# Turned shares and key shifts in one PSUM bank, shares ahead of numbers, batch norm in one ScalarE step

## The chip, the core and the metric

One core of a Trainium2 chip runs the kernel. Its engines are TensorE (PE, with the weight load PEld beside it), VectorE (DVE), ScalarE (ACT), GpSimd (POOL) and SyncE (SP), which here only issues transfers. The metric is the device time of one execution in microseconds (us), as the median of several runs. A profile is one further execution, recorded by the hardware profiler.

## The reference

```python
x = L0_attn_x                                         # 16 x 512 x 128
x = x + attention(layernorm(x), w_qkv, w_proj)        # 16 heads of 8, window of 128
y = layernorm(x)                                      # input of the experts
mu, var = mean(y, 0), mean((y - mu) ** 2, 0)          # over all 8192 tokens
q = ((y - mu) * rsqrt(var + 1e-5) * gamma + beta) @ w_q.T
sim = einsum('pbnhd,hkpd->pbnhk', q, keys)            # 8 heads, 2 x 32 keys
s, i = top_k(sim, 8)                                  # for both halves of the keys
scores, pk = top_k(sx[:, None] + sy[None, :], 8)      # 8 of the 64 sums
idx = take(ix * 32 + iy, pk)                          # 8 of 1024 experts a head
o = gelu(y . key_in[idx]) * softmax(scores)
return x + sum(o * key_out[idx])
```

## The kernel before, in words

The first part is the windowed attention of the sixteen batches, followed by the second layer norm, whose transposed output goes to DRAM. The change doesn't touch it.

The second part starts with the batch norm: `bn_aggr` (L547) gives mean and variance of each of the 128 features, L549 to L551 make `bn_a` = gamma / sqrt(var + eps), a value for each partition.

Then come the experts. A batch has 512 tokens, in four tiles of 128, so there are 64 turns of the main loop (L872); turn i works on tile t = i mod 4 of batch b. The order of instructions on each of the four compute engines is written out by hand: `InOrder` (its calls all carry line L577) keeps every engine's instructions in the order of the program text. The loop overlaps three turns: it finishes turn i - 1, works on i, and begins i + 1. In one turn:

- `where_keys` (sixteen MAX8 and FIND_INDEX8 results of the two key halves of 8 heads), `best_sums` and `where_sums` (L674) find the eight best sums of each head and the place of each among 64. `where_sums` splits the place into `upper` and `shift`: two VectorE steps for each, on 64 elements a partition.
- `pick_words` (L693) picks the word that holds the key's number on GpSimd; `share_of` (L700) makes the softmax shares: VectorE sums and inverts, GpSimd multiplies (`share`).
- `numbers` (L709) shifts `word` by `shift` on VectorE and takes three fields out of it (`num`, three VectorE steps). It stands between the first four and the last twelve of the sixteen MAX8 of turn i + 1 (`best_keys`, L630).
- `turn` (L719) casts `num` to bf16 on ScalarE and turns shares and numbers round on TensorE, so that choices lie on partitions: two fp32 matmuls for the shares into columns 2, six bf16 ones into columns 0 and 1 of `x_ps`. ScalarE then copies `p_bf` and `wT` out.
- `other_ones_of_p` (L766), `ones_of_c` (L744), `weights_at_c` (L752) and `ones_of_p` (L759) build one-hot rows (`row`) and weighted columns (`mine`, `cols`) on ScalarE, VectorE and GpSimd; `weigh` (L781) multiplies them on TensorE into `w_ps`, the weight of every expert for every token.
- `take_weights` and `weigh_experts` multiply these by the GELU of `down`; `up` (L807) multiplies the product by `key_out`.

`fill(i, 0)` and `fill(i, 1)` (L851) put the matmuls of other batches between: in odd turns `down` of the batch that follows, with its GELUs on ScalarE; in even turns `up` of a batch that came before. `fill(i, 0)` stands ahead of `where_sums`, so its matmuls are ahead of `turn`'s in TensorE's queue. `scale` (L594) applies the batch norm to a batch, at the end of turn t = 2 of the batch before.

`x_ps` is in the pool `ps_t` (L562), one buffer of one PSUM bank; VectorE reads it in `ones_of_c` and `ones_of_p`.

Of the kernel before, what the change touches and what calls it, by code (L numbers as in the profile page):

```python
# [10 lines left out]
F32 = mybir.dt.float32  # L11
BF16 = mybir.dt.bfloat16
I32 = mybir.dt.int32
U32 = mybir.dt.uint32
U8 = mybir.dt.uint8
AF = mybir.ActivationFunctionType
ALU = mybir.AluOpType
# [3 lines left out]
P = 128  # L21
# [22 lines left out]
def kernel(  # L44
# [13 lines left out]
    nc = tc.nc  # L58
# [12 lines left out]
    const = ctx.enter_context(tc.tile_pool(name="const", bufs=1))  # L71
# [9 lines left out]
    for b in range(B):  # L81
        t = keep.tile([P, NQ, D], F32, name=f"x_{b}")
# [3 lines left out]
    gb = const.tile([P, 2], F32, name="gb")  # L86
# [8 lines left out]
    ident = const.tile([P, P], F32, name="ident")  # L95
    make_identity(nc, ident)
    ident_bf = const.tile([P, P], BF16, name="ident_bf")
# [42 lines left out]
    xts = {}  # L140

    def load(b):
        xts[b] = ahead.tile([P, T], F32, tag="xt", name=f"xt_{b}")
        nc.sync.dma_start(xts[b], xT[b])
# [8 lines left out]
    with ExitStack() as at:  # L153
# [280 lines left out]
        def weigh(n, u):  # L434

            b, g = divmod(n, NG)
            ts = near(u)
            q0, w = ts[0] * P, len(ts) * P
            pT = probs.pop((n, u))
            if u == 0:  # L440
                outs[n] = ps_o.tile([P, T], F32, tag="o", name=f"o_ps_{n}")
            for j in range(4):
                mm(
                    outs[n][32 * j : 32 * j + 32, q0 : q0 + w], lhsT=vaug[b % 3][:, u, 4 * g + j],
                    rhs=pT[:, j, 0:w], start=u == 0, stop=u == NQ - 1, skip_group_check=True,
                )
            if u == NQ - 1:
                oT = w2.tile([P, T], F32, tag="oT", name=f"oT_{n}")
                nc.scalar.copy(oT, outs[n])
                outs[n] = oT  # L450
# [46 lines left out]
        for s in range(-2 * NG * NQ, (NU + 1) * NQ):  # L497
            n, u = divmod(s, NQ)
            b, g = divmod(n, NG)
# [46 lines left out]
    bn_mv = const.tile([P, 2], F32, name="bn_mv")  # L546
    nc.vector.bn_aggr(bn_mv, bn_st.rearrange("p b s -> p (b s)"))  # L547
    bn_a = const.tile([P, 1], F32, name="bn_a")
    nc.scalar.activation(bn_a, bn_mv[:, 1:2], AF.Sqrt, bias=eps)  # L549
    nc.vector.reciprocal(bn_a, bn_a)  # L550
    nc.vector.tensor_mul(bn_a, bn_a, gb[:, 0:1])  # L551

# [2 lines left out]
    b2 = ctx.enter_context(tc.tile_pool(name="b2", bufs=2))  # L557
# [4 lines left out]
    ps_t = ctx.enter_context(tc.tile_pool(name="ps_t", bufs=1, space=PSUM))  # L562
    HK = H * TOPK
    HT, QT = P // 2, P // 4
    NM = QT // 2
    HM = NM // 2
    halves = [slice(v * HT, v * HT + HT) for v in range(2)]
# [11 lines left out]
    pe, dve, act, pool = (InOrder(e) for e in (nc.tensor, nc.vector, nc.scalar, nc.gpsimd))  # L579
# [9 lines left out]
    xbs, downs, gels, gs, ups, outs_T = {}, {}, {}, {}, {}, {}  # L589
    sims, tops, cands, idxs, bytes_of, steps_of = {}, {}, {}, {}, {}, {}  # L590
    bests, ws, shares, places, shifts, words, nums, turned = {}, {}, {}, {}, {}, {}, {}, {}
    mines, rows, weights = {}, {}, {}

    def scale(b):  # L594
        xb = b2.tile([P, T], F32, tag="xb", name=f"xb_{b}")
        dve.tensor_scalar(xb, xts[b], bn_mv[:, 0:1], bn_a, ALU.subtract, ALU.mult)
        act.activation(xb, xb, AF.Identity, bias=gb[:, 1:2])
        xbs[b] = xb

    def down(b, k):  # L600
# [16 lines left out]
    def score(j):  # L617
        b, t = divmod(j, NQ)
        sims[j] = ps_x.tile([P, 2 * H, NK], F32, tag="x", name=f"sim_ps_{j}")
        pe.matmul(  # L620
            sims[j].rearrange("p c k -> p (c k)"), lhsT=xbs[b][:, t * P : (t + 1) * P], rhs=wsim,
            start=True, stop=True,
        )

    def take_scores(j):
        sim = b2.tile([P, 2 * H, NK], F32, tag="sim", name=f"sim_{j}")
        act.copy(sim, sims[j])
        sims[j] = sim
# [16 lines left out]
    def where_keys(j):  # L645
        idx = b2.tile([P, H, 2, TOPK], U32, tag="idx", name=f"idx_{j}")
        sim, top = sims.pop(j), tops.pop(j)
        for c in range(2 * H):
            dve.max_index(idx[:, c // 2, c % 2], top[:, c // 2, c % 2], sim[:, c])
        idxs[j] = idx  # L650
# [23 lines left out]
    def where_sums(j):  # L674
        place = b2.tile([P, H, TOPK], U32, tag="place", name=f"place_{j}")
        best, cand = bests.pop(j), cands.pop(j)
        for h in range(H):
            dve.max_index(place[:, h], best[:, h], cand[:, h].rearrange("p a b -> p (a b)"))

        place = place.rearrange("p h k -> p (h k)")  # L680
        upper = b2.tile([P, 2, HK], U32, tag="upper", name=f"upper_{j}")
        shift = b2.tile([P, 2, HK], U32, tag="shift", name=f"shift_{j}")
        for i, right in enumerate((5, 2)):
            dve.tensor_scalar(
                upper[:, i], place, right, 1, ALU.logical_shift_right, ALU.bitwise_and
            )
        places[j], shifts[j] = upper, shift
        for i, left in enumerate((0, 3)):
            dve.tensor_scalar(
                shift[:, i], place, left, 24, ALU.logical_shift_left, ALU.bitwise_and  # L690
            )
# [8 lines left out]
    def share_of(j):  # L700
# [5 lines left out]
        pool.tensor_tensor(share, w, bc(zs, 2, TOPK), ALU.mult)  # L706
        shares[j] = share

    def numbers(j):  # L709

        key = words.pop(j).rearrange("p s h k -> p s (h k)").bitcast(U32)
        dve.tensor_tensor(key, key, shifts.pop(j), ALU.logical_shift_right)
        num = b2.tile([P, 3, HK], U32, tag="num", name=f"num_{j}")
        dve.tensor_scalar(num[:, 0], key[:, 0], NK - 1, 5, ALU.bitwise_and, ALU.logical_shift_left)
        dve.tensor_scalar(num[:, 1], key[:, 1], NC, None, ALU.bitwise_and)
        dve.tensor_scalar(num[:, 2], key[:, 1], NC - 1, None, ALU.bitwise_and)
        nums[j] = num

    def turn(j):  # L719

        num = b2.tile([P, 3, HK], BF16, tag="num_bf", name=f"num_bf_{j}")
        act.copy(num, nums.pop(j))
        x_ps = ps_t.tile([P, 3, HT], F32, tag="t", name=f"x_ps_{j}")
        share = shares.pop(j).rearrange("p h k -> p (h k)")
        for i, (to, what, eye) in enumerate((
            (2, share, ident), (0, num[:, 0], ident_bf), (0, num[:, 1], ident_bf),
            (1, num[:, 2], ident_bf),
        )):
            for v in range(2):
                pe.matmul(  # L730
                    x_ps[halves[v], to], lhsT=what, rhs=eye[:, halves[v]],
                    start=i == 0, stop=i != 1, skip_group_check=True,
                )
        p_bf = b2.tile([P, HT], BF16, tag="p_bf", name=f"p_bf_{j}")
        act.copy(p_bf, x_ps[:, 0])
        wT = b2.tile([P, HT], F32, tag="wT", name=f"wT_{j}")
        act.copy(wT, x_ps[:, 2])
        turned[j] = x_ps, p_bf, wT

    def some(t, m, rows_of=slice(0, P)):  # L740

# [52 lines left out]
    def take_weights(j, m):  # L794
        b, t = divmod(j, NQ)
        if t == m == 0:
            gs[b] = b2.tile([P, NC, NQ, 2, QT], F32, tag="g", name=f"g_{b}")
        g = gs[b][:, :, t, :, m * NM : m * NM + NM]
        act.copy(g, weights.pop((j, m)).rearrange("p n (s c) -> p c s n", s=2))
# [72 lines left out]
    for i in range(NB + 1):  # L872
        b, t = divmod(i, NQ)
        now, before, behind = i < NB, i > 0, i + 1 < NB
        if now:
            where_keys(i)
            if t == 0 and 0 < b < B - 1:
                load(b + 1)
        if behind:
            score(i + 1)  # L880
        if before:
            take_weights(i - 1, 0)
            weigh(i - 1, 1)
        if now:
            pack_keys(i)
        if behind:
            take_scores(i + 1)
        if now:
            best_sums(i)
            less_greatest(i)  # L890
        if before:
            weigh_experts(i - 1, 0)
            take_weights(i - 1, 1)
        if i == 0:
            for k in range(3, 8):
                down(0, k)
                gelu(0, k)
        if t == 1 and b > 1:
            finish(b - 2)
        fill(i, 0)  # L900
        if now:
            where_sums(i)
            pick_words(i)
            share_of(i)
        if t == 1 and b > 1:
            store(b - 2)
        if before:
            weigh_experts(i - 1, 1)
        if not now:
            break  # L910
        tops_of = best_keys(i + 1) if behind else iter(())
        next(tops_of, None)
        numbers(i)
        for _ in tops_of:
            pass
        turn(i)
        other_ones_of_p(i, 0)
        ones_of_c(i)
        if behind:
            sums_of_keys(i + 1)  # L920
        weights_at_c(i, 0)
        ones_of_p(i, 0)
        other_ones_of_p(i, 1)
        ones_of_p(i, 1)
        weights_at_c(i, 1)
        fill(i, 1)
        weigh(i, 0)
        if t == 2 and b + 1 < B:
            scale(b + 1)
# [41 lines left out]
```

## Time and profile before

| | |
|---|---|
| median of 3 runs | 1741.71 us (1736.61 to 1748.68) |
| the profiled execution: time, span | 1729.36 us, 1727.7 us |
| granted TensorE clock in it | 0.971 |
| busy over the span | PE 1447.6, PEld 851.4, DVE 1414.8, ACT 1175.8, POOL 1138.2 us |
| busy from 837.0 us to the end (890.7 us) | PE 752.7, PEld 522.4, DVE 835.5, ACT 657.2, POOL 605.4 us |
| `row<-x_ps,nums_p` on DVE | 128 times, 1214 ns each |
| `mine<-x_ps,nums_c` on DVE | 64 times, 1225 ns each |
| `upper<-place` on DVE | 128 times, 295 ns each |
| `cols<-mine,wT` on POOL | 256 times, 1066 ns each |
| `g<-g,gel` on POOL | 128 times, 1296 ns each |
| `wT<-x_ps` on ACT | 64 times, 218 ns each |
| `xb<-xt,bn_mv,bn_a` on DVE | 16 times, 589 ns each |
| `xb<-xb,gb` on ACT | 16 times, 705 ns each |

How to read it: a row of the profile names the line (L577 for all that `InOrder` records, so tiles tell them apart), the engine, the operation, what it writes and reads (`out<-in`), its shapes and types, and how often (x). In a list of groups, behind the bar, stand the busy time in us and the mean in ns of one, and then the idle time of the engine just before them with the releaser that ended it. In a timeline the first two columns are the start and the time taken, in us from the start of the span; neighbours of one kind are merged into one row. A list of waits has the waiting engine and tile, whom it waited for, and the total in us, the number of waits and the longest. In the page's slices each digit is a fortieth of the span in tenths of busy time, or, for PEclk, of the full clock that was granted.

### The profile page before, as it was taken

To read this page: it belongs to the slowest core of one execution; us is meant where nothing else is said; L and a number is where in the kernel's file an instruction comes from. 1 tells how busy PE (TensorE), PEld (TensorE's weight loads), DVE (VectorE), ACT (ScalarE), POOL (GpSimd) and SP (SyncE) were. 2 spreads that over 40 slices of the span, in tenths; PEclk is the share of its full clock that TensorE was granted. 3 is DMA by queue.
4 is the path that set the end of the run, shared out by engine and by line. 5 is a ranking of instruction groups with operands and counts; after the bars stand their busy time and mean duration, and the time that the engine had idled before them with its cause. 6 is when DMAs were issued, how large, how long until landed. Compare 5 with 4: busy or idle time off the path is not lost.

```text
span 1727.7 us, 49763 instructions
## 1 busy us (share of the span) xinstructions
PE 1447.6 (84%) x16752; PEld 851.4 (49%) x16752; DVE 1414.8 (82%) x7959; ACT 1175.8 (68%) x2530; POOL 1138.2 (66%) x1762
## 2 busy tenths in 40 slices
PE   4789898798788898898678888888888888888887
PEld 1344443344344443443345656565565655655655
DVE  3767777677776776684599999899999999999994
ACT  1466667666666666667577777777777777777773
POOL 9556557865577557646376766676767777676764
PEclk9799999999999999999899999899999999999998
DMA  6242222222222222221000000000000000000000
GB/s 168 70 112 83 72 76 65 81 75 72 69 72 82 76 71 68 78 70 38 20 8 2 14 14 9 14 8 15 14 8 15 8 15 14 9 15 8 8 9 14
DMA packets 87567, 75.05 MB, mean 43 GB/s; under 512 B 12176, under 2 KB 83088, under 8 KB 87184
## 3 DMA queue, kind: packets, MB, share of 16 engines
q1 hardware_dynamic: 86480, 71.61, 14.0%
q8 instruction: 133, 2.18, 0.5%
q14 instruction: 122, 1.00, 0.2%
q10 hardware_dynamic: 832, 0.26, 0.1%
HBM read 49.28 MB, written 20.97 MB: 41 GB/s over the span
## 4 chain that ended last, share of the span: by engine, by line
PE 35%; DVE 24%; ACT 22%; POOL 6%; SPq 6%; issue 4%; DMA 3%; DVEq 0%; ACTq 0%; POOLq 0%
PE s_ps L168 6%; PE o_ps L168 6%; PE w_ps L577 6%; ACT row L577 5%; DVE masked L379 4%; ACT off_p L577 4%; SPq L354 4%; PE e_ps L168 4%; ACT L577 3%; PE sim_ps L577 3%; DVE idx L577 3%; DVE num L577 3%; PE dn_ps L577 3%; DVE row L577 3%; ACT pT L421 3%
## 5 line engine op out<-in xcount | busy, mean ns | idle before, releaser
L379 DVE CUSTOM_DVE_ANT_0 masked<-s_ps,band 128x384 bf16<-128x384 f32 (+1 forms) x1024 | 498.8, 487 | 215.0 <-PE s_ps L168 83.2
L421 ACT ACTIVATE pT<-e_ps 128x384 f32<-128x384 f32 (+1 forms) x1024 | 389.5, 436 | 161.1 <-PE e_ps L168 156.9
L428 POOL TENSOR_SCALAR_AFFINE_SELECT pT<-pT 128x512 f32<-128x512 f32 x384 | 236.7, 635 | 232.6 <-ACT pT L421 228.1
L168 PE MATMUL s_ps<-kst,qst 128*128 128x384 bf16 (+1 forms) x1024 | 312.5, 308 | 36.4 <-DVE mx L379 17.8
L577 PEld LDWEIGHTS w_ps<-cols,row 128*64 128x64 f32 x8192 | 256.2, 140 | 90.9 <-POOL cols L577 38.1
L577 POOL TENSOR_TENSOR cols<-mine,wT 64x512 f32<-64x512 bf16 x256 | 272.9, 1066 | 35.3 <-DVE mine L577 22.0
L577 PE MATMUL w_ps<-cols,row 128*64 128x32 f32 x8192 | 266.3, 224 | 22.5 <-POOL cols L577 20.6
L168 PE MATMUL e_ps<-qst,kst 128*128 128x384 bf16 (+1 forms) x1024 | 230.3, 304 | 14.7 <-ACT pT L421 12.4
L168 PEld LDWEIGHTS <-qst 128*128 128x128 bf16 x1024 | 101.1, 99 | 211.3 <-issue 165.7
L168 PE MATMUL o_ps<-pT,vaug 128*32 128x384 f32 (+1 forms) x2048 | 193.4, 450 | 13.1 <-POOL pT L428 12.9
L577 ACT ACTIVATE row<-off_p,one 128x512 f32<-128x512 bf16 x256 | 184.8, 722 | 8.3
L577 ACT ACTIVATE off_p<-off_ps 128x512 bf16<-128x512 f32 x256 | 149.0, 582 | 37.9 <-PE off_ps L577 37.9
L577 POOL TENSOR_TENSOR g<-g,gel 128x512 f32<-128x512 f32 x128 | 165.9, 1296 | 5.1 <-ACT g L577 5.1
L577 DVE FIND_INDEX8 idx<-top,sim 128x8 uint32<-128x32 f32 x1024 | 166.2, 184 | 0.0
L577 DVE TENSOR_TENSOR row<-x_ps,nums_p 128x1024 f32<-128x1024 f32 x128 | 150.0, 1214 | 0.0
L577 PE MATMUL dn_ps<-xt,key_inT 128*64 128x256 f32 x1024 | 128.8, 396 | 20.8 <-ACT off_p L577 19.4
L577 PE MATMUL off_ps<-p_bf,ident_bf 128*128 128x512 bf16 x256 | 100.2, 391 | 46.5 <-ACT off_p L577 27.0
L577 POOL TENSOR_TENSOR cand<-top 128x512 f32<-128x512 f32 x64 | 68.1, 1065 | 98.2 <-DVE top L577 98.2
L577 PE MATMUL up_ps<-g,key_out_sb 64*128 64x256 f32 x1024 | 126.8, 388 | 0.0
L168 PEld LDWEIGHTS <-kst 128*128 128x128 bf16 x1024 | 98.1, 98 | 55.5 <-issue 29.1
L577 DVE MAX8 top<-sim 128x8 f32<-128x32 f32 x1024 | 104.5, 171 | 3.6 <-ACT sim L577 3.6
L577 PEld LDWEIGHTS dn_ps<-xt,key_inT 128*64 128x64 f32 x1024 | 70.2, 141 | 70.9 <-ACT off_p L577 34.2
(141 smaller groups left out, 2461.2 us busy)
## 6 DMA issues: line engine op xcount, KB each, us to landing
qst<-qv SPq DMA_DIRECT2D x576, 32.0 KB
kst<-kv SPq DMA_DIRECT2D x576, 32.0 KB
qv<-qp SPq DMA_DIRECT2D x16, 384.0 KB
kv<-kp SPq DMA_DIRECT2D x16, 384.0 KB
x<-in_L_attn_x_dram SPq DMA_DIRECT2D x16, 256.0 KB
xT<-xiT SPq DMA_DIRECT2D x16, 256.0 KB
xt<-xT SPq DMA_DIRECT2D x16, 256.0 KB
out_dram<-o_sb SPq DMA_DIRECT2D x16, 256.0 KB
```

What stands on the lines that cost most here:

```text
L168: tc.keep_in_program_order(nc.tensor.matmul(*args, **kw))
L354: nc.sync.dma_start(st[r : r + DK], src[i if what == "q" else j, :, 4 * g : 4 * g + 4])
L379: nc.vector.tensor_tensor_reduce(masked[:, 0:w], s, band.rearrange("p u k -> p (u k)")[:, from_u : from_u + w], 1.0, LOWEST, ALU.add, ALU. ...
L421: nc.scalar.activation(pT[:, h, 0:w], e_ps[:, 0:w], AF.Exp)
L428: nc.gpsimd.affine_select(out=side, in_=side, compare_op=ALU.is_ge, fill=0.0, base=0, pattern=[[0, 4], [sign, P]], channel_multiplier=-sign,)
L577: return lambda *args, **kw: tc.keep_in_program_order(op(*args, **kw))
```

## The change

Three things are done.

1. The tile `x_ps` is made in `where_sums`, as eight groups of 64 columns[...]. `shift` is no longer an SBUF tile: it is columns 3 and 4 of that bank, and `numbers` writes the shifted words there too, over the shifts, and reads its three fields from there.
2. The two fp32 matmuls of the shares and the copy `wT` leave `turn` and become `turn_shares`, called just ahead of `numbers`. `turn` keeps the six matmuls of the numbers, none of which starts the bank anew, and the copy `p_bf`.
3. `scale` is one ScalarE activation with a scale and a bias for each partition, in place of a VectorE step and a ScalarE step. For that `bn_b` = beta - mean * bn_a is made once, in two small VectorE steps.

```diff
     nc.vector.tensor_mul(bn_a, bn_a, gb[:, 0:1])
+    bn_b = const.tile([P, 1], F32, name="bn_b")
+    nc.vector.tensor_mul(bn_b, bn_mv[:, 0:1], bn_a)
+    nc.vector.tensor_sub(bn_b, gb[:, 1:2], bn_b)
...
     def scale(b):
         xb = b2.tile([P, T], F32, tag="xb", name=f"xb_{b}")
-        dve.tensor_scalar(xb, xts[b], bn_mv[:, 0:1], bn_a, ALU.subtract, ALU.mult)
-        act.activation(xb, xb, AF.Identity, bias=gb[:, 1:2])
+        act.activation(xb, xts[b], AF.Identity, bias=bn_b, scale=bn_a)
         xbs[b] = xb
...
         upper = b2.tile([P, 2, HK], U32, tag="upper", name=f"upper_{j}")
-        shift = b2.tile([P, 2, HK], U32, tag="shift", name=f"shift_{j}")
+
+        turned[j] = ps_t.tile([P, 8, HT], F32, tag="t", name=f"x_ps_{j}")
+        shift = turned[j][:, 3:5].bitcast(U32)
...
+    def turn_shares(j):
+
+        share = shares.pop(j).rearrange("p h k -> p (h k)")
+        for v in range(2):
+            pe.matmul(
+                turned[j][halves[v], 2], lhsT=share, rhs=ident[:, halves[v]],
+                start=True, stop=True, skip_group_check=True,
+            )
+        wTs[j] = b2.tile([P, HT], F32, tag="wT", name=f"wT_{j}")
+        act.copy(wTs[j], turned[j][:, 2])
+
     def numbers(j):
 
-        key = words.pop(j).rearrange("p s h k -> p s (h k)").bitcast(U32)
-        dve.tensor_tensor(key, key, shifts.pop(j), ALU.logical_shift_right)
+        key = shifts.pop(j)
+        word = words.pop(j).rearrange("p s h k -> p s (h k)").bitcast(U32)
+        dve.tensor_tensor(key, word, key, ALU.logical_shift_right)
         num = b2.tile([P, 3, HK], U32, tag="num", name=f"num_{j}")
         dve.tensor_scalar(num[:, 0], key[:, 0], NK - 1, 5, ALU.bitwise_and, ALU.logical_shift_left)
...
-        x_ps = ps_t.tile([P, 3, HT], F32, tag="t", name=f"x_ps_{j}")
-        share = shares.pop(j).rearrange("p h k -> p (h k)")
-        for i, (to, what, eye) in enumerate((
-            (2, share, ident), (0, num[:, 0], ident_bf), (0, num[:, 1], ident_bf),
-            (1, num[:, 2], ident_bf),
-        )):
+        x_ps = turned[j]
+        for i, (to, what) in enumerate(((0, num[:, 0]), (0, num[:, 1]), (1, num[:, 2]))):
             for v in range(2):
                 pe.matmul(
-                    x_ps[halves[v], to], lhsT=what, rhs=eye[:, halves[v]],
-                    start=i == 0, stop=i != 1, skip_group_check=True,
+                    x_ps[halves[v], to], lhsT=what, rhs=ident_bf[:, halves[v]],
+                    start=False, stop=i != 0, skip_group_check=True,
                 )
         p_bf = b2.tile([P, HT], BF16, tag="p_bf", name=f"p_bf_{j}")
         act.copy(p_bf, x_ps[:, 0])
-        wT = b2.tile([P, HT], F32, tag="wT", name=f"wT_{j}")
-        act.copy(wT, x_ps[:, 2])
-        turned[j] = x_ps, p_bf, wT
+        turned[j] = x_ps, p_bf, wTs.pop(j)
...
         next(tops_of, None)
+        turn_shares(i)
         numbers(i)
```

More of the change, by code (lines that the diff above doesn't have):

```diff
@@ L591 @@
     bests, ws, shares, places, shifts, words, nums, turned = {}, {}, {}, {}, {}, {}, {}, {}
-    mines, rows, weights = {}, {}, {}
+    mines, rows, weights, wTs = {}, {}, {}, {}
     def scale(b):
         xb = b2.tile([P, T], F32, tag="xb", name=f"xb_{b}")
-        dve.tensor_scalar(xb, xts[b], bn_mv[:, 0:1], bn_a, ALU.subtract, ALU.mult)
-        act.activation(xb, xb, AF.Identity, bias=gb[:, 1:2])
+        act.activation(xb, xts[b], AF.Identity, bias=bn_b, scale=bn_a)
         xbs[b] = xb
```

## The prediction, made before the changed kernel ran

> **What bounds the kernel now.** I read first the page's span, slices and clock, to see where the change lies.
>
> ```profile
> span 1727.7 us, 49763 instructions
> ...
> DVE  3767777677776776684599999899999999999994
> ...
> PEclk9799999999999999999899999899999999999998
> ```
>
> Every edited line belongs to the second half, the experts, which starts with the batch norm at 837 us and holds 64 turns of one loop. There VectorE (DVE) is at nine tenths or more in nearly every slice, and the clock is close to full. That says "VectorE bounds it", but a full engine may be full of waiting, so I read next the groups by shape from 740 us on.
>
> ```profile
> L577 DVE TENSOR_SCALAR num<-word 128x64 uint32<-128x64 uint32 x192 | 70.5, 421 | 2.2
> ...
> L577 DVE TENSOR_TENSOR word<-word,shift 128x128 uint32<-128x128 uint32 x64 | 35.0, 546 | 4.1 <-POOL word L577 4.0
> ...
> L577 DVE TENSOR_SCALAR shift<-place 128x64 uint32<-128x64 uint32 x128 | 18.3, 184 | 0.0
> ```
>
> `num` and `shift` are the same operation on the same 64 elements, yet take 421 and 184 ns. The timeline of one turn tells why (times in us: start, duration). This is turn t=2 of a batch:
>
> ```profile
> 1202.71 2.06 PE L577 MATMUL w_ps<-cols,row 128*64 128x32 f32 x64
> ...
> 1204.70 2.86 PE L577 MATMUL up_ps<-g,key_out_sb 64*128 64x256 f32 x24
> ...
> 1205.38 0.42 DVE L577 MAX8 top<-sim 128x8 f32<-128x32 f32 x4
> 1205.60 0.30 POOL L577 TENSOR_TENSOR share<-w,zs 128x64 f32<-128x64 f32 x1
> 1205.71 0.33 DVE L577 TENSOR_TENSOR word<-word,shift 128x128 uint32<-128x128 uint32 x1
> 1205.85 1.32 POOL L577 TENSOR_TENSOR g<-g,gel 128x512 f32<-128x512 f32 x1
> 1206.08 1.35 DVE L577 TENSOR_SCALAR num<-word 128x64 uint32<-128x64 uint32 x3
> 1207.36 1.21 DVE L577 MAX8 top<-sim 128x8 f32<-128x32 f32 x12
> 1207.47 0.35 ACT L577 CAST num_bf<-num 128x192 bf16<-128x192 uint32 x1 [2.02 <-DVE num L577]
> 1207.49 0.20 PEld L577 LDWEIGHTS x_ps<-ident,share 128*64 128x64 f32 x4 [0.33 <-POOL g L577]
> 1207.49 0.34 PE L577 MATMUL x_ps<-ident,share 128*64 128x64 f32 x4
> ...
> 1208.31 0.22 ACT L577 COPY wT<-x_ps 128x64 f32<-128x64 f32 x1
> ```
>
> Two things are to be seen. First, GpSimd's `g` (1205.85 to 1207.17) stands over `num`: three instructions that take 0.40 elsewhere (at 1193.62) end only as `g` does. Second, and this decides: the shares are ready on GpSimd at 1205.90, but TensorE (PE) turns them at 1207.49 to 1207.83, because the `up` matmuls of `fill(i, 0)` stand ahead of them in its queue. The turned shares can't exist before 1207.83. `num` ends at 1207.43, its cast at 1207.82: VectorE, ScalarE (ACT) and PE meet there within 0.05 us. So the stage is VectorE-full and at the same time a loop of latencies that has no slack at this point.
>
> **The change part by part.**
>
> *Numbers from PSUM (the gain).* `word` and `num` hold VectorE 35.0 + 70.5 = 105.5 us. Afterwards `key` and `shift` are in the bank of `x_ps`. [...] My uncontended price: `word` 0.33, its successor 0.04 later, three `num` 0.40 as at 1193.62[...]. Sum 0.87 us. Lower bound 0.77 (no PSUM toll); upper bound 1.1, from the reciprocal that reads PSUM (`rec<-t_ps`, 254 ns) against the one in SBUF (`zs`, 203 ns): 50 ns for each of four. So VectorE is relieved of 105.5 - 64 x 0.87 = 50 us.
>
> *Shares turned and copied first (the price).* In the built program, PE's order is unchanged: the share matmuls stand behind the `dn` or `up` matmuls of `fill(i, 0)` as before. What is new is that `wT`, a ScalarE read of the bank, comes ahead of `numbers`, whose first instruction now writes that bank; VectorE waits for ScalarE's `wT` just before `word`. [...] The trace has a row for such a wait: from 760 to 1700 us,
>
> ```profile
> DVE mine L577 <- ACT wT L577: 11.2, 4, 5.1
> ```
>
> VectorE's `mine` waits for ScalarE's `wT`, though both only read the bank and at different columns. [...] Guarded by address, shifts (columns 3 and 4) and shares (column 2) are apart, numbers wait for nothing new, and the sum would be at most -50. Guarded by bank, `numbers` starts only after PE's share matmuls and ScalarE's copy. The built program has the second.
>
> Cost per turn; always end of the previous `num` to end of this one:
> - t=2 (and t=0, alike). Previous end 1193.62 + 0.40 = 1194.02. Share matmuls end 1207.83, that is 13.81 later. Then `wT`: 0.05 until ScalarE starts (as before `p_bf`), 0.22, 0.03 until VectorE starts: 1208.13. Then 0.87: 1209.00 in place of 1207.43. **+1.57**.
> - t=3. Share matmuls end 1220.38 + 0.28 = 1220.66, but ScalarE is in `gelu` until 1219.88 + 1.08 = 1220.96, ahead of `wT` in its queue. So 1220.96 + 0.03 + 0.22 + 0.03 + 0.87 = 1222.11 in place of 1219.47 + 1.36 = 1220.83. **+1.28**.
> - t=1. Share matmuls end 1247.16 + 0.28 = 1247.44, gelu 1247.11. 1247.44 + 0.30 + 0.87 = 1248.61 in place of 1247.44. **+1.17**.
>
> Does the next turn absorb it? What follows hangs on the end of `num`: the cast, six matmuls, `p_bf`, `off_ps`, four Square/Relu pairs on ScalarE and, behind twelve MAX8, `mine` and the GpSimd `cols`; then PE's `w_ps` (1212.10, held by POOL `cols` for 0.69) and from there PE back to back: `w_ps`, `sim_ps`, `w_ps`, `dn`, shares. Queued behind the waiting `word` are those twelve MAX8 (1.21 us), so `mine`, `row` and GpSimd's `cand` go late with it. Nothing in this string starts from another anchor. So the loop grows by the full amount: 2 x 1.57 + 1.28 + 1.17 = 5.59 us a batch. Thirteen batches (2 to 14) give 72.7. In batches 0, 1 and 15 some turns have no `up` or no `dn` ahead of the shares; the same working on their turns gives 3.9, 4.2 and 3.0. Sum **+84**. The 50 us of relief are already inside it, as the 0.87.
>
> *Scale in one step.* 16 VectorE instructions of 589 ns go, 9.4 us. ScalarE's stays one of 705 ns. The relief falls in t=2 just before VectorE waits over a microsecond for `wT`: worth nothing, but -9.4 if VectorE were the bound. The first one is on the path: the 1.38 us at 837.31 go and two 0.16 us operations with 0.04 gaps come: **-1**, once.
>
> *At nothing.* The `shift` pair in PSUM [...]: hidden by VectorE's new wait[...]. Moving `wT` from behind `p_bf`: its old place lay in the 0.57 that ScalarE waits for `off_ps`, so no gain. No DMA and no step on SP or GpSimd moves; GpSimd's order is the same.
>
> **Sum.** 84 - 1 = 83 on the profiled execution: 1729.4 to 1812. The three runs' median is 1741.7, 12 above that execution; I add 83 to it: **1825 us**, 4.8% slower.
>
> **Rivals.**
> - *Numbers don't wait in effect, and the relief shows* (not slower). It needs `wT` done before the first four MAX8 end, 1205.80 at t=2, so share matmuls done by 1205.5, 2.3 us earlier than the trace has them. For it: shares are ready at 1205.90, nearly so. Against: the `up` matmuls are in PE's queue ahead. It decides only if these ran later than the shares. Even then PE and ScalarE free at 1207.83 allow some 0.3 us in t=1 and 0.1 elsewhere, 64 x 0.15 = 10 us; with VectorE's full relief -60. 1682 to 1732.
> - *The loop gives half back.* PE's string holds two waits of its own: 0.69 for POOL `cols` (1212.10) after an even turn, 0.65 for ACT `off_p` after an odd one. If they shrink once VectorE's number steps no longer contend with GpSimd, up to 0.65 x 64 = 42 come back: 1783. Against: `cols` and `off_p` run a microsecond and more after these steps.
> - *More than the sum.* At 980 to 1000 us the granted clock was 0.87, and `dn` took 3.68 in place of 2.8; VectorE's bound hid part of that, and a PE loop shows all. With the upper bound 1.1 (+15) and some microseconds for each such stretch: +110, 1852.
>
> **Chances.** Forecast 0.73, half back 0.11, more 0.10, not slower 0.06. The forecast's own range: 0.77 to 1.1 in place of 0.87 is -6 to +15, and the runs of before spread by 12: 1808 to 1848. To leave out no more than 2 in 10 I go down to 1796. About 1% is what a measurement of this kernel can tell from no change; of the 0.06, half lies within it: faster 0.03, same 0.03, slower 0.94.
>
> **What would show it.** Right: VectorE idle before `word` (or the `x_ps` it then writes), put down to ACT `wT`, about 1.9 to 2.4 us a turn; `num` down from 421 to under 220 ns; a turn of 14.7 in place of 13.4; VectorE's digits from 9 to 8; first four MAX8 unchanged, the other twelve after the wait. Wrong: a wait under 1 us, share matmuls that start earlier against the previous `num`, or `num` still above 300 ns.

## The result, and the profile after

| | before | changed |
|---|---|---|
| median of 4 runs | 1740.61 us (1736.61 to 1748.68) | 1870.46 us (1867.58 to 1882.56) |
| ratio, 95% interval | 1 | 1.0753 (1.0692 to 1.0814) |
| span of the profiled execution | 1727.7 us | 1865.6 us |
| granted clock: whole span, from 837 us on | 0.971, 0.97 | 0.915, 0.87 |

The changed kernel is 7.5% slower: 130 us where 83 were forecast. The direction and the mechanism were forecast; the time lies above the range. The page's slices, to be held against those of before:

```profile
span 1865.6 us, 49812 instructions
...
DVE  3767777777767767828776787887868868876884
...
PEclk9899999999999999989797797988979979987989
```

VectorE is down from nine tenths to seven or eight, as forecast. The last row was not: the clock of TensorE, nearly full before in the second half, now dips every few slices down to seven tenths. In the helper's new numbering, `InOrder` is L580. The groups from 740 us on:

```profile
L580 DVE TENSOR_SCALAR num<-x_ps 128x64 uint32<-128x64 uint32 x192 | 31.2, 218 | 2.3
...
L580 DVE TENSOR_TENSOR x_ps<-word,x_ps 128x128 uint32<-128x128 uint32 x64 | 19.0, 296 | 166.6 <-ACT wT L580 166.6
```

`num` fell from 421 to 218 ns and the shift of the words from 546 to 296: 105.5 us became 50.2. This alone does not show that the bank gave the relief, because the new wait also moves `num` out of GpSimd's way: only 7 of its 192 steps now run beside a GpSimd instruction, where 94 did before. The run with PSUM alone, below, settles it. Behind the second bar stands what the change costs VectorE: 166.6 us idle ahead of the shift, all ended by ScalarE's `wT`. The timeline of a turn t=0 at full clock shows the string that was worked out beforehand:

```profile
1103.22 0.30 POOL L580 TENSOR_TENSOR share<-w,zs 128x64 f32<-128x64 f32 x1
...
1105.10 0.34 PE L580 MATMUL x_ps<-ident,share 128*64 128x64 f32 x4
1105.48 0.21 ACT L580 COPY wT<-x_ps 128x64 f32<-128x64 f32 x1 [2.42 <-PE x_ps L580]
1105.80 0.29 DVE L580 TENSOR_TENSOR x_ps<-word,x_ps 128x128 uint32<-128x128 uint32 x1 [2.39 <-ACT wT L580]
1106.13 0.49 DVE L580 TENSOR_SCALAR num<-x_ps 128x64 uint32<-128x64 uint32 x3
1106.53 1.21 DVE L580 MAX8 top<-sim 128x8 f32<-128x32 f32 x12
1106.65 0.35 ACT L580 CAST num_bf<-num 128x192 bf16<-128x192 uint32 x1 [0.95 <-DVE num L580]
...
1107.06 0.28 PE L580 MATMUL x_ps<-ident_bf,num_bf 128*64 128x64 bf16 x6 [1.62 <-ACT num_bf L580]
```

The shares are ready at 1103.52; TensorE, with `up` ahead of them, turns them at 1105.10; VectorE sits idle for 2.39 us and starts at 1105.80. The last line holds what the prediction passed over: TensorE itself now stands idle for 1.62 us between the shares and the numbers. Before, in the turn that the prediction shows, the shares ran from 1207.49 to 1207.83 and the numbers followed with no wait:

```profile
1207.87 0.28 PE L577 MATMUL x_ps<-ident_bf,num_bf 128*64 128x64 bf16 x6
```

**Where the time went.** For turns 8 to 59, thirteen whole batches, I take the time from the end of one `num` to the end of the next out of the timeline, once as the sum over all of them and once as thirteen times the four turns t=0 to t=3 at full clock. The difference is what the clock took. In the changed kernel no turn t=3, and so no batch, ran at full clock from end to end; its figure for t=3 is the shortest such turn. The kernel with two fillers below ran all of these turns at full clock and has the same four figures to 0.01 us.

| kernel | t=0, 1, 2, 3 at full clock, us | 13 such batches | turns 8 to 59 | lost to the clock |
|---|---|---|---|---|
| before | 13.41, 13.20, 13.41, 13.39 | 694.3 | 701.5 | 7 |
| changed | 14.98, 14.28, 14.98, 14.65 | 765.6 | 825.8 | 60 |

So of 124 us in these turns, 71 are the wait and its loop (72.7 were forecast), and 53 are the clock (the forecast had no term for it). The turns outside them add 14 of the span's 138.

### The profile page after: what moved, and what is told of

The parts are those of the page before. It is cut to its first block, busy times and chain, and to the rows that moved or that the text cites. A ratio compares the mean times of both kernels' runs of the same rounds, so it can differ in the third digit from the quotient of the medians.

```text
span 1865.6 us, 49812 instructions
## 1 busy us (share of the span) xinstructions
PE 1540.6 (83%) x16752; PEld 898.6 (48%) x16752; DVE 1370.5 (73%) x7945; ACT 1185.0 (64%) x2530; POOL 1134.0 (61%) x1762
## 4 chain that ended last, share of the span: by engine, by line
PE 54%; ACT 15%; DVE 12%; POOL 8%; SPq 5%; issue 4%; DMA 2%; DVEq 0%; ACTq 0%; POOLq 0%
PE w_ps L580 13%; PE up_ps L580 7%; PE o_ps L168 6%; PE s_ps L168 6%; PE dn_ps L580 4%; PE sim_ps L580 4%; DVE masked L379 4%; PE e_ps L168 4%; PE off_ps L580 4%; SPq L354 4%; ACT off_p L580 3%; ACT row L580 3%; ACT pT L421 2%; POOL xi L292 2%; DVE num L580 2%
## 5 line engine op out<-in xcount | busy, mean ns | idle before, releaser
L580 PEld LDWEIGHTS w_ps<-cols,row 128*64 128x64 f32 x8192 | 279.9, 150 | 83.2 <-issue 48.0
L580 PE MATMUL w_ps<-cols,row 128*64 128x32 f32 x8192 | 289.4, 233 | 8.1 <-POOL cols L580 8.1
L580 POOL TENSOR_TENSOR cols<-mine,wT 64x512 f32<-64x512 bf16 x256 | 269.8, 1054 | 20.0 <-DVE mine L580 2.9
L580 POOL TENSOR_TENSOR cand<-top 128x512 f32<-128x512 f32 x64 | 68.3, 1067 | 208.9 <-DVE top L580 208.9
L580 ACT ACTIVATE row<-off_p,one 128x512 f32<-128x512 bf16 x256 | 184.8, 722 | 8.4
L580 ACT ACTIVATE off_p<-off_ps 128x512 bf16<-128x512 f32 x256 | 149.1, 583 | 50.8 <-PE off_ps L580 50.8
L580 POOL TENSOR_TENSOR g<-g,gel 128x512 f32<-128x512 f32 x128 | 163.9, 1281 | 10.8 <-ACT g L580 10.8
L580 DVE FIND_INDEX8 idx<-top,sim 128x8 uint32<-128x32 f32 x1024 | 166.3, 186 | 0.0
L580 PE MATMUL off_ps<-p_bf,ident_bf 128*128 128x512 bf16 x256 | 123.0, 480 | 37.5 <-ACT p_bf L580 19.5
L580 DVE TENSOR_TENSOR row<-x_ps,nums_p 128x1024 f32<-128x1024 f32 x128 | 150.1, 1215 | 0.0
L580 PE MATMUL up_ps<-g,key_out_sb 64*128 64x256 f32 x1024 | 147.8, 436 | 0.0
L580 PE MATMUL dn_ps<-xt,key_inT 128*64 128x256 f32 x1024 | 134.7, 409 | 15.1 <-ACT off_p L580 13.7
L580 DVE TENSOR_TENSOR x_ps<-word,x_ps 128x128 uint32<-128x128 uint32 x64 | 19.0, 296 | 166.6 <-ACT wT L580 166.6
L580 PE MATMUL off_ps<-less_nums,ident_bf 128*128 128x512 bf16 x256 | 125.6, 490 | 0.0
L580 PEld LDWEIGHTS up_ps<-g,key_out_sb 64*128 64x128 f32 x1024 | 108.4, 216 | 34.8 <-issue 20.0
```

The source lines that it names most:

```text
L580: return lambda *args, **kw: tc.keep_in_program_order(op(*args, **kw))
```

## The experiments

Theory: `numbers` writes the bank that `wT` reads, so VectorE waits for the copy and the whole loop grows by 5.5 us a batch; the pause that this opens on TensorE makes its granted clock fall to half in stretches, and that is the rest. Rivals: the new place of the shares costs it whatever the bank; steps on PSUM cost it; the clock fell for another reason. Each kernel was measured beside the kernel before on the same chip, whose medians were 1728 to 1741, so the ratios are to be compared.

### Is it the pause on TensorE that lowers the clock?

In the traces of the kernel before and of the changed one, each stretch of one clock (30 and 96 of them) lasts a whole number of 3.41 us, but for the last, which the end of the kernel cuts off. A view of busy time, laid on these steps of the clock, shows what comes before a fall. The columns are TensorE's busy us and instructions, the granted clock, and DMA:

```profile
1112.64:1116.05 3.41, 3.41 (x86) 1.00 0.00 0
1116.05:1119.47 3.42, 3.42 (x38) 1.00 0.18 52
1119.47:1122.88 3.41, 1.49 (x16) 1.00 0.10 29
1122.88:1139.94 17.06, 16.35 (x159) 0.50 0.01 1
```

Two stretches of 3.41 us are full; the third holds the pause and is busy for 1.49; the clock is 0.50 for the next 17.06 us, although TensorE is busy for 16.35 of them. The fall thus follows a stretch that was 44% busy, with a pause of 1.62 us in it (ahead of the numbers at 1121.34).

So far the pause and the fall only coincide; to test for a cause, work was put into the pause: six matmuls whose result nothing reads (a filler).

```diff
     def turn_shares(j):
...
+        fill_ps = ps_x.tile([P, HM, NP], F32, tag="x", name=f"fill_ps_{j}")
+        for _ in range(6):
+            pe.matmul(fill_ps, lhsT=ident_bf, rhs=bc(less_nums, 1, HM), start=True, stop=True)
```

> The changed kernel with six idle-time matmuls of 128x512 bf16 (0.21 us each) on TensorE right behind the share matmuls, into a buffer that nothing reads: work is added, results stay. Theory (the 1.6 us gap on TensorE behind the shares lowers the granted clock, and that is what the prediction lacked): clock of the second half from 0.87 to 0.96 or more, turns of 15.0, 14.7 and 14.3 us without the long ones of 21.6, time 1870 - 45 = 1825. Rival (the clock falls for another reason, such as heat or more work in flight): clock 0.87 or lower, 1870 or more.

Measured: ratio 1.0568 (1.0520 to 1.0617), 1839 us, clock from 837 us on 0.95. The turns at full clock are the same to 0.01 us (14.98, 14.28, 14.98, 14.65), and of the 60 us lost to the clock 31 are left. Those fell nearly all in t=3, after TensorE's waits for `cols` and for `xb` (0.58 and 0.86 us idle; the profile puts the second down to `best`, but `xb` ended at 1070.63, just before the matmul at 1070.68). So four more such matmuls were put there:

```diff
+            if t == 3:
+                idle_ps = ps_x.tile([P, HM, NP], F32, tag="x", name=f"idle_ps_{i}")
+                for _ in range(4):
+                    pe.matmul(idle_ps, lhsT=ident_bf, rhs=bc(less_nums, 1, HM), start=True, stop=True)
             score(i + 1)
```

> The changed kernel with the six filler matmuls behind the shares and four more ahead of the sim_ps matmul of turns t=3, where TensorE waits for xb: the gap at which the clock still fell with the first filler. Nothing reads what they write. Theory (gaps on TensorE lower the clock; the wait for the bank is worth 84 us): no long turns are left in the middle batches, clock of the second half 0.98, all turns at 14.98, 14.28, 14.98, 14.65 us, time 1812 to 1825. Rival (the clock falls for another reason and the first filler helped by chance): as with one filler, 1839 or more, with long turns somewhere else.

Measured: ratio 1.0460 (1.0429 to 1.0491), 1809.8 us. TensorE's rows of one turn, and then the second half of the changed kernel and of this one (busy us and instructions of PE, PEld, DVE, ACT, POOL, then clock and DMA):

```profile
1057.94 0.34 PE L580 MATMUL x_ps<-ident,share 128*64 128x64 f32 x4
1058.21 1.47 PE L580 MATMUL fill_ps<-less_nums,ident_bf 128*128 128x512 bf16 x6
1059.89 0.28 PE L580 MATMUL x_ps<-ident_bf,num_bf 128*64 128x64 bf16 x6 [0.22 <-ACT num_bf L580]
```

```profile
837.00:1866.00 1029.00, 846.68 (x11584) 569.92 (x11584) 790.36 (x5456) 665.77 (x1248) 598.74 (x770) 0.87 0.03 10
837.00:1807.00 970.00, 848.89 (x12028) 557.61 (x12028) 783.48 (x5456) 663.53 (x1248) 598.02 (x770) 0.99 0.04 10
```

The pause is 0.22, the clock 0.99, the thirteen batches take 765.9 us, which is 0.3 above full clock, and no long turn is left. With 444 matmuls more in the second half than it needs (12028 where the changed kernel has 11584), the kernel is 2.7% faster than the changed one (1.0460 over 1.0753). So in these turns it is the pauses that lower the clock; under the rival, heat or more work in flight, it would have stayed at 0.87 or fallen further, and it rose to 0.99. What is left, 765.9 - 701.5 + 7 = 71 us, is the wait.

### Is the wait one for the bank?

The shares were turned into a buffer of `ps_x`, in a bank of their own, at the same place on every engine.

```diff
+        s_ps = ps_x.tile([P, HM, NP], F32, tag="x", name=f"share_ps_{j}")
         for v in range(2):
             pe.matmul(
-                turned[j][halves[v], 2], lhsT=share, rhs=ident[:, halves[v]],
+                s_ps[halves[v], 0], lhsT=share, rhs=ident[:, halves[v]],
...
-        act.copy(wTs[j], turned[j][:, 2])
+        act.copy(wTs[j], s_ps[:, 0])
...
-                    start=False, stop=i != 0, skip_group_check=True,
+                    start=i == 0, stop=i != 0, skip_group_check=True,
```

The last line follows from the first: the shares no longer start the bank of the numbers, so the numbers do.

> The changed kernel with one thing undone: the shares are turned into a buffer of the pool ps_x, a bank of their own, so that wT reads another bank than numbers writes; their place ahead of the numbers stays on every engine. Theory (the shared bank makes the wait): VectorE's 166 us of waiting for wT vanish, num stays near 220 ns, turns fall from 15.0 to 13.6 or less (as with the shares ahead alone) and the clock returns to 0.97: 1715 to 1745. Rival (the new place of the shares is the price): 1825 to 1870.

Measured: ratio 1.0195 (1.0158 to 1.0231), 1762 us. VectorE's waits from 837 us on no longer name `wT`:

```profile
DVE mine L580 <- ACT p_bf L580: 89.9, 61, 5.3
```

The wait for the bank is gone, and with it three quarters of the loss; thirteen batches take 714.0 us, 2 of them lost to the clock. The forecast was a little too good. In these turns 12.5 us are left, because `wT` still stands ahead of the cast `num_bf` on ScalarE (VectorE now waits for `p_bf`, two steps on). Another 17 lie in the first and last batches. There the clock is at half for 68 us in all, against 32 in the kernel before; half of the difference, 18 us, is an estimate of what that can cost. TensorE's wait of 1.18 us for GpSimd's `share`, with no `up` or `dn` in front, stands ahead of the first such stretches in both kernels; why they last 17 us here and 7 before is open.

The opposite test leaves the shared bank and puts the copy back behind `p_bf`:

```diff
     def turn_shares(j):
...
-        act.copy(wTs[j], turned[j][:, 2])
...
         act.copy(p_bf, x_ps[:, 0])
+        act.copy(wT, x_ps[:, 2])
```

> The changed kernel with the share matmuls ahead of the numbers as there, but the copy wT behind p_bf as before. Theory (the wait is for the bank, whoever uses it): numbers now wait for TensorE's share matmuls in place of the copy, 0.25 us less a turn, turns of 14.7, 14.0, 14.7, 14.1 at full clock, clock still low, 1830 to 1860. Rival (the wait is for the copy): VectorE's wait gone, 1715 to 1740.

Measured: ratio 1.0473 (1.0400 to 1.0546), 1817 us; turns 14.73, 14.13, 14.73, 14.26. From 837 us on:

```profile
DVE x_ps L580 <- PE x_ps L580: 142.9, 62, 7.3
```

VectorE now waits for TensorE's writes to the bank in place of the copy, 0.26 us less a turn, as expected. So the wait is for the bank, whoever uses it. Better than expected is the total: the pause on TensorE is shorter,

```profile
1207.26 0.28 PE L580 MATMUL x_ps<-ident_bf,num_bf 128*64 128x64 bf16 x6 [1.37 <-ACT num_bf L580]
```

and the turns 8 to 59 lose 16 us to the clock in place of 60. A quarter of a microsecond goes with most of that loss; the last section shows how.

### The parts alone

Shares ahead, with shifts and words in SBUF and `x_ps` made in `turn_shares`:

> The kernel before with the second part alone: shares turned and copied ahead of the numbers, shifts and words in SBUF. Theory: numbers touch no bank and wait for nothing new, but on ScalarE the cast of the numbers now stands behind wT, which waits for TensorE: +0.65 us in turns t=0 and t=2, +0.35 in t=3, +0.27 in t=1, so 1.9 a batch, +28 us and some more where the longer gap on TensorE lowers the clock: 1765 to 1790. Rival (the move of the shares is the price, whatever the bank): as the changed kernel, 1825 to 1870. Rival 2 (only the bank matters): 1740.

Measured: ratio 1.0043 (1.0026 to 1.0060), 1745 us. Below the range: with the cast behind `wT`, TensorE pauses ahead of the numbers for 0.56 to 0.70 us in every turn (before, for 0.45 and 0.59 in the odd ones alone),

```profile
1219.14 0.28 PE L577 MATMUL x_ps<-ident_bf,num_bf 128*64 128x64 bf16 x6 [0.70 <-ACT num_bf L577]
```

but a batch grows by 1.1 us (13.62, 13.61, 13.53, 13.79) in place of 1.9, and none of its thirteen batches lost anything to the clock. The place of the shares alone is thus worth some 0.4%, not 7.5.

PSUM alone, with the shares behind the numbers:

```diff
-        shift = b2.tile([P, 2, HK], U32, tag="shift", name=f"shift_{j}")
+        turned[j] = ps_t.tile([P, 8, HT], F32, tag="t", name=f"x_ps_{j}")
+        shift = turned[j][:, 3:5].bitcast(U32)
...
-        dve.tensor_tensor(key, key, shifts.pop(j), ALU.logical_shift_right)
+        dve.tensor_tensor(key, word, key, ALU.logical_shift_right)
...
-        x_ps = ps_t.tile([P, 3, HT], F32, tag="t", name=f"x_ps_{j}")
+        x_ps = turned[j]
```

> The kernel before with the first part alone: shifts and shifted words in the bank of x_ps, shares still turned behind the numbers. Theory (the price is VectorE's wait for the copy wT, and the PE gap behind it): num falls from 421 to about 220 ns and word to about 300, VectorE gets no new wait, and the time hardly moves because TensorE's up or dn matmuls and ScalarE's GELU hold the turn: 1725 to 1742, clock as before (0.97). Rival 1 (VectorE alone was the bound): 50 us faster, 1690. Rival 2 (steps on PSUM are themselves dear): 1780 or more.

Measured: ratio 0.9893 (0.9861 to 0.9926), 1715 us: faster than before, and more than expected. `num` is at 218 ns here too, although 180 of its 192 steps run beside a GpSimd instruction. None of the 192 takes over 225 ns; in the kernel before, the 94 beside one took 665 in the median, and the other 98 took 185. So the relief does come from the bank, and neither steps on PSUM nor a shared bank as such is dear: the shift of the words no longer waits for any other engine's use of the bank (0.3 us of waits in all, for GpSimd's `word`). VectorE is busy for 47 us less from 837 us on (788.5 in place of 835.5), and the kernel is only 18 us shorter in the profiles, because TensorE holds the turns: even in t=0 and t=2 the shares come right behind `up`. The rest VectorE spends waiting, 49.4 us ahead of `mine` for `wT` in place of 12.4. What I had missed is a part of the old distance, 0.38 us from shares to numbers, which falls to 0.16 once the cast is ready in time:

```profile
1189.82 2.86 PE L577 MATMUL up_ps<-g,key_out_sb 64*128 64x256 f32 x24
1192.62 0.34 PE L577 MATMUL x_ps<-ident,share 128*64 128x64 f32 x4
1192.78 0.26 PE L577 MATMUL x_ps<-ident_bf,num_bf 128*64 128x64 bf16 x6
```

In t=1 it falls by 0.49, as TensorE's pause for the cast is gone; in t=3 it stays. Together that is 0.93 of the 1.0 us by which a batch is shorter.

The batch norm in one step, alone:

> The kernel before with the third part alone: batch norm in one ScalarE step. Theory (turns are held by TensorE and ScalarE as much as by VectorE): 1 to 4 us faster, 1737 to 1740. Rival (VectorE alone is the bound): 9 us faster, 1731.

Measured: ratio 1.0055 (1.0034 to 1.0076), 1747 us: slower, where 1 to 4 us faster were expected. VectorE's step is gone (t=3 takes 12.94 in place of 13.39), but the turn behind it takes 13.95 in place of 13.41. The `sim_ps` matmul waits for ScalarE's `xb`, and that got longer, from 706 to 798 ns (before, then this run):

```profile
L577 ACT ACTIVATE xb<-xb,gb 128x512 f32<-128x512 f32 x16 | 11.3, 706 | 2.2 <-DVE xb L577 2.2
L580 ACT ACTIVATE xb<-xt,bn_b,bn_a 128x512 f32<-128x512 f32 x15 | 12.0, 798 | 0.0
```

The step with a bias and a scale takes 92 ns more than the one with a bias alone, and the prediction left that out. At full clock a batch is longer by 0.1 us, only 1.6 us in all; of the 14 us by which the profiles differ, 12 are the clock (19 us lost in the thirteen batches in place of 7). Which pause makes it fall here was not tested.

### A version that beats both

Since TensorE's queue ahead of the shares holds the turns after the relief, half of the six `up` steps of `fill(i, 0)` in even turns were moved to `fill(i, 1)`.

```diff
-                up(b - 2, range(8, 14) if place == 0 else range(14, NC))
+                up(b - 2, range(8, 11) if place == 0 else range(11, NC))
...
-            up(b - 1, range(6) if place == 0 else range(6, 8))
+            up(b - 1, range(3) if place == 0 else range(3, 8))
```

> The first part alone (shifts and words in PSUM, shares behind the numbers as before) and in even turns half of the six up steps of fill(i, 0) moved to fill(i, 1), so that TensorE reaches the shares 1.4 us earlier. Theory (with VectorE relieved, TensorE's queue ahead of the shares holds the even turns): 0.7 us less in each of 32 even turns, 22 us, from 1715 to 1693, unless the gap ahead of the numbers' matmuls lowers the clock and takes it back. Rival (VectorE or ScalarE holds the turn after the relief): 1715 as without.

> The kernel before with only that move of half of the up steps in even turns. Theory (VectorE, TensorE and ScalarE meet within 0.05 us at the numbers, so VectorE holds the turn as soon as TensorE is early): same time within 5 us, 1735 to 1745. Rival (TensorE alone holds it): 20 us faster.

Both of these kernels leave out three of the sixteen `up` steps of the last batch but one, since the end of the loop skips them. Measured: with PSUM 0.9813 (0.9785 to 0.9842), 1697 us; on the kernel before alone 1.0046 (1.0021 to 1.0070), 1739 us, its turns unchanged (13.41, 13.21, 13.46, 13.38) and 14 us lost to the clock in place of 7. With the three steps behind the loop as well:

```diff
-    up(B - 2, range(14, NC))
+    up(B - 2, range(11, NC))
```

> Shifts and words in PSUM, shares behind the numbers, half of the even turns' up steps moved to fill(i, 1), now with the last batches' up steps complete after the loop. Theory (VectorE relieved and TensorE's queue shorter ahead of the shares, both are needed): turns at 13.4, 12.7, 13.0, 12.4, 1695 to 1702. Rival (the gain came from the three steps that were missing): 1710 or more.

Measured: ratio 0.9800 (0.9749 to 0.9852), 1698.7 us; turns 13.43, 12.71, 13.04, 12.44, none lost to the clock in turns 8 to 59. So neither relief alone gives this: the split alone gains nothing, since an early TensorE finds VectorE late, and PSUM alone gains 1.1%, since an early VectorE finds TensorE late. Together they give 2.0% (1.5 to 2.5), and the time that VectorE was relieved of is no longer mere slack.

| kernel | at full clock | 13 such batches | turns 8 to 59 | lost to the clock | ratio |
|---|---|---|---|---|---|
| one filler | 14.98, 14.28, 14.98, 14.65 | 765.6 | 796.7 | 31 | 1.0568 |
| two fillers | the same | 765.6 | 765.9 | 0 | 1.0460 |
| copy behind | 14.73, 14.13, 14.73, 14.26 | 752.1 | 767.8 | 16 | 1.0473 |
| other bank | 14.22, 13.82, 13.33, 13.43 | 712.4 | 714.0 | 2 | 1.0195 |
| shares ahead alone | 13.62, 13.61, 13.53, 13.79 | 709.2 | 709.2 | 0 | 1.0043 |
| scale alone | 13.95, 13.21, 13.41, 12.94 | 695.6 | 714.8 | 19 | 1.0055 |
| PSUM alone | 13.42, 13.17, 12.71, 13.12 | 681.5 | 689.9 | 8 | 0.9893 |
| PSUM and split | 13.43, 12.71, 13.04, 12.44 | 671.1 | 671.5 | 0 | 0.9800 |

## Why the prediction was right in the mechanism and wrong in the size

- **The wait of VectorE for `wT`**: right, in place and price. 14.98, 14.28, 14.98 and 14.65 us a turn were measured; the working gave 13.41 + 1.57 = 14.98, 14.37, 14.98 and 14.67. Other bank (no wait for `wT` ahead of the shift) and copy behind (142.9 us of waits for TensorE's writes) show that it is the bank.
- **Numbers from PSUM at 0.87 us**: 1105.80 to 1106.62, 0.82. Right, though no trace of before shows the part of the working between 0.77 and 0.87, nor that these steps don't contend with GpSimd once they are in PSUM. The runs show both: with PSUM alone a `num` takes 216 ns in the median, beside GpSimd or not, and before, with no GpSimd instruction beside it, 185: 31 ns less.
- **Nothing absorbs it**: right; with the clock held up, 71 us came where 72.7 were worked out. That the relief of VectorE without the wait would be worth some 10 us was half of what PSUM alone gave (18 in the profiles).
- **Scale**: its relief is worth nothing, as said. "ScalarE's stays one of 705 ns" was wrong: 800.
- **At nothing**: `upper`, which is not edited, went from 295 to 375 ns. It lies ahead of VectorE's wait and is covered.
- **The step that failed is the sum**: "83 on the profiled execution". It took every TensorE duration from a trace at a clock of 0.97 and put them into a loop with a new pause on TensorE, so the clock had no term in it. The prediction followed what is late behind VectorE's wait (MAX8, `mine`, `cand`) and had TensorE's restart at the cast in its own string, but did not ask what TensorE does meanwhile. The rival "more than the sum" named the clock, but gave it some microseconds for stretches that were there before. What the runs showed in place of that term: the clock fell to half at pauses in every batch, which took 53 us more than before in the thirteen batches, and 44 of 60 us lost went when the pause was a quarter of a microsecond shorter, all of them when the pauses were filled.
- **The rival "half back"** is refuted: with the first pause filled, TensorE still waits 0.58 us for `cols` (0.69 before) and 0.65 for `off_p` (0.65), and 71 of 72.7 us came.

## What to carry to other kernels

When two engines use one PSUM bank, look for the wait that orders them before counting what the operands' place saves: the same PSUM steps gained 1% with no other engine's use ahead of them, and the change as a whole cost 7.5% with such a use put ahead. When a change opens a pause on TensorE, price the pause twice: its length, and the clock at which everything behind it then runs; here a pause of 1.6 to 1.8 us in each turn cost 53 us through the clock, and the wait that opened it 71. And before counting on a relief, see whether another engine arrives at the same point: here two of them had to be relieved together.

## What the hardware showed that I had not expected

In the changed kernel a pause of 1.62 us was enough to halve the clock. Laid on the steps of the clock, turns 8 to 59 hold 33 stretches of 3.41 us at full clock in which TensorE was busy for less than half of the time. After 32 of them the clock was halved; after the 146 busier ones it never was. The pause of 1.37 us in the copy-behind kernel leaves TensorE busy for 51% of such a stretch, just on the other side: of 22 stretches like that, 4 were followed by the half clock. So a quarter of a microsecond can weigh as much as it does here.

Half busy does not tell every fall. With one filler eight falls are left, after stretches that were 61 to 70% busy, and the kernel before has such falls too (TensorE's busy us and instructions, clock, DMA):

```profile
1100.53:1103.94 3.41, 2.12 (x65) 1.00 0.02 5
1103.94:1114.18 10.24, 10.24 (x90) 0.50 0.01 2
```

These are 62%, while other stretches of that kernel, 55% busy, kept the full clock. What tells them apart is open, and so is why some falls of the changed kernel last for one stretch and others for five or six: from 1122.88 us on the clock stayed at half for 17.06 us of nearly unbroken work (16.35 us busy).
